# Gate products side by side, the convolutions' end spread over steps, and result rows in 4 KB pieces

## The chip, the cores and the metric

The kernel runs on one core of one Trainium2 chip. The metric is device time in microseconds (us) for one execution, lower is better. The core has five engines with an instruction queue each, and each works through its queue in order: TensorE (PE, matrix products; its weight loads are shown apart as PEld), VectorE (DVE), ScalarE (ACT), GpSimd (POOL) and SyncE (SP, which here only issues transfers). Matrix products land in PSUM, of which this kernel uses eight tiles of 128 x 512 float32 in turn; all other tiles lie in SBUF. The engines wait for one another by semaphores, and 16 DMA engines move data between HBM and SBUF. Everything is float32.

## The reference, cut to what matters

Four images of 256 channels and 32 x 32 places (1024 tokens each) pass through a "metaformer" layer and then through a mixture of eight experts, of which each token uses two.

```python
def _L0_conv_ref(x, ...):
    xn = layernorm(xs, norm_w, norm_b)                     # per token, over 256 channels
    xm = mamba_v(xc, ...) + skip_scale * xc                # 4 groups of 64 channels: a scan over 1024 tokens
    Q = conv1d(conv1d(x_concat, qdw_w, qdw_b, groups=NB, pad=1), qpw_w, qpw_b, groups=1, pad=0)
    g = jax.nn.sigmoid(Q)                                  # 4 gates per token
    xg = (g[...] * xm) ...                                 # each group of 64 channels times its gate
    R = conv1d(conv1d(xgt, rdw_w, rdw_b, groups=Cc, pad=1), rpw_w, rpw_b, ...) + xgt
    cat = concatenate([xs, R])
    xm2 = conv1d(conv1d(cat, fdw_w, fdw_b, groups=2 * Cc, pad=1), fpw_w, fpw_b, ...) + cat[:, :Cc, :]
    x_local = conv1d(xm2, lc_w, lc_b, groups=Cc, pad=1)
    x_global = mha(xm2, ...)                               # 8 heads
    x_out = gelu(layernorm(concatenate([x_local, x_global]) @ fc_w.T + fc_b, lgn_w, lgn_b))
    ...                                                    # depthwise 3x3, norm, projection

x = x + _L0_conv_ref(_ln_c(x), ...)
t = _to_tokens(x)
t = t + _L0_ffn_ref(_ln_t(t), ...)     # top 2 of 8 experts, each gelu(x W1 + b1) W2 + b2
x = _from_tokens(t, x)
```

The first convolution of `Q` takes three neighbouring tokens and the 64 channels of a group to one value per group, so 256 channels to 4; the second takes 4 to 4.

## The kernel before

The program is one interleaving made by hand. Pieces of work are Python generators; `yield n` says "go on n steps later", and `beat()` lets one step pass. A step of the scan is one pair of DVE instructions (`dBu`, then the scan `hs`), a part is 16 steps (one group of one image, one half of its tokens), and an image has eight parts. I write part 1.2 for part 2 of image 1. While image b is scanned in parts b.0 to b.3, `convolutions(b - 1)` runs beside it; after part b.3 the scan pauses for `attention(b - 1)`. The last image's convolutions, attention and norms run after the scan, between tiles of the experts (256 rows each); the remaining tiles follow, and `bring_back` ends the program.

```python
        def step(b, n, h, i):                                   # one step of the scan
            dBu = ps(...)
            nc.vector.tensor_tensor(dBu, dts[g][:, 1, :], bs[q], ALU.mult)
            nc.vector.tensor_tensor_scan(hs, dA[i], dBu, 0.0 if h == 0 else last, ALU.mult, ALU.add)
            ...
            nc.gpsimd.tensor_tensor(hs, hs, cs[q], ALU.mult)
        # dA is made on ACT three steps ahead (LEAD = 3); bs on PE from step g == 1 of the quarter before
        # yp (sums of hs) on PE; up, zp, dtp, cp, op are the projections of the neighbouring parts
...
        def in_turn(items, make, use, lag=2):
            made = []
            for at in range(len(items) + lag):
                if at >= lag:
                    use(items[at - lag], made[at - lag])
                if at < len(items):
                    made.append(make(items[at]))
                yield 1
...
        def normalised(b):
            ...
            for c in range(NC2):
                xl = a4(f"xl_{b}_{c}")
                nc.gpsimd.tensor_tensor(xl, xn[:, c, LEFT:], r1, ALU.mult)
                yield 1
                nc.vector.tensor_tensor(xn[:, c, LEFT:], xn[:, c, LEFT:], r2, ALU.mult)
                ...
        def convolutions(b):
            ...                                                  # d[0]: depthwise of xs, for fp
            qs, qd = [], []
            for h in range(2):
                qd.append(ps(f"qd_{b}_{h}"))
                for i in range(6):
                    c, k = divmod(i, 3)
                    nc.tensor.matmul(
                        qd[h][0:NB], qdwT_s[:, c, k, :], xm[:, c, ds(k + h * HALF, HALF)],
                        start=(i == 0), stop=(i == 5),
                    )
                    if i % 3 == 2:
                        yield 1
            for h in range(2):
                yield 1 - h
                qs.append(a2(f"qs_{b}_{h}", NB))
                nc.scalar.activation(qs[h], qd[h][0:NB], AF.Identity, bias=...)
            yield 1
            # gate(c): gp = qpwT_s x qs, two products of 4 rows; sigmoid(c, gp): g on ACT, with a table
            # load before and after; then xm = g * xm (POOL), depthwise d[1] of xm (ACT, DVE, DVE),
            # rp = rpwT x d[1] (PE) added to xm (DVE), depthwise d4r of xm, and then:
            yield from in_turn(
                CO_H, lambda at: product(f"fp_...", fpwT_s, at[0], [...]), mixed,
            )                                                     # 4 items of 4 products; mixed: DVE
            yield from prepared(b)                                # vp and qkp, for the attention
...
    def bring_back(self, b, m2):
        y = m2.tile([P, NT, C], F32, tag="yy", name=f"yy_{b}", bufs=self.B)
        for h in range(2):
            nc.sync.dma_start(
                y[:, ts(h, NT // 2), :],
                self.Y[ds(b * N + h * HALF, HALF), :].rearrange("(t p) c -> p t c", p=P),
            )
        o = m2.tile([P, NC2, N], F32, tag="o", name=f"o_{b}")    # two buffers
        for h in range(2):
            for c in range(NC2):
                op = self.psum.tile(...)
                for t in range(NT // 2):
                    nc.tensor.transpose(op[:, ts(t, P)], y[:, h * (NT // 2) + t, ts(c, P)], self.ident)
                if c: nc.scalar.copy(o[:, c, ts(h, HALF)], op)
                else: nc.vector.tensor_copy(o[:, c, ts(h, HALF)], op)
            nc.scalar.dma_start(self.out[b]..., o[:, :, ts(h, HALF)])
```

## Time and profile before

| | |
|---|---|
| time | 2474.78 us, median of 3 runs (2465.03 to 2476.65) |
| span of the profiled execution | 2472.8 us |
| scan and what lies beside it | 60.6 to 1657.9 us |
| last image's convolutions to routing, with expert tiles between | 1657.9 to about 2145 us |
| expert tiles alone | about 2145 to 2436 us |
| loading, turning and storing the result | 2436 to 2472.8 us |
| busy over the span | PE 2134.3, DVE 1632.3, ACT 1194.4, POOL 1101.3 us |
| mean granted clock of PE | 0.906 |

A line of the timeline gives start, duration, engine, source line, operation, output and inputs, shapes, and in brackets how long the engine had been idle before and what released it. A line of the windows gives a stretch, its length, the busy time of PE, PEld, DVE, ACT and POOL with the number of instructions, the granted PE clock, the busy share of the DMA engines and what they moved. A float32 product shows as two records, so "x8" is four products. A busy PE is not a PE at its peak, and a wait for several semaphores is put down to the one that the profile shows last.

### The profile page before, as it was taken

The numbers are of one execution on the slowest core, as the hardware profiler recorded it, in microseconds if no ns is written. First come the engines' busy times: TensorE is split into PE (matmuls) and PEld (weight loads), VectorE is DVE, ScalarE is ACT, GpSimd is POOL, SyncE is SP. The second block draws the span as 40 slices with busy tenths as digits, with TensorE's granted clock in tenths as the row PEclk, the third lists the DMA queues.
The fourth block names the chain that finished last, engine by engine and source line by source line (L and its number), as shares of the span: only waits on it lengthen the run. The fifth ranks groups of instructions, "written<-read, shape, count | busy, mean of one in ns | idle before, by whom it ended". The sixth has DMA issues, their size and how long they took to land. (4 is left out here: it accounts for less than half of the span.)

```text
span 2472.8 us, 28317 instructions
## 1 busy us (share of the span) xinstructions
PE 2134.3 (86%) x8810; PEld 947.7 (38%) x8810; DVE 1632.3 (66%) x2255; ACT 1194.4 (48%) x2019; POOL 1101.3 (45%) x1182
## 2 busy tenths in 40 slices
PE   7767768999977799987689999658999889899995
PEld 2111112322211132222123223114752568788885
DVE  3989898875898977789878787985525154211111
ACT  4554445468654548764254786325258533122221
POOL 0777776632676850366776205571130012322221
PEclk7888888899998899988788999768999989899997
DMA  3534433220334230043322202342340155766665
GB/s 90 138 99 111 99 95 78 60 56 27 74 94 108 72 76 26 22 115 91 112 74 57 48 18 59 88 154 88 90 124 1 45 152 162 211 197 193 193 197 157
DMA packets 154980, 244.30 MB, mean 99 GB/s; under 512 B 34184, under 2 KB 103452, under 8 KB 154816
## 3 DMA queue, kind: packets, MB, share of 16 engines
q1 hardware_dynamic: 135640, 217.05, 31.0%
q0 software_dynamic: 13264, 17.85, 3.7%
q10 hardware_dynamic: 5912, 7.45, 0.9%
q8 instruction: 74, 1.21, 0.2%
q14 instruction: 90, 0.74, 0.1%
HBM read 141.16 MB, written 33.98 MB: 71 GB/s over the span
## 5 line engine op out<-in xcount | busy, mean ns | idle before, releaser
L607 POOL TENSOR_TENSOR hs<-hs,cs 128x512 f32<-128x512 f32 x512 | 669.6, 1309 | 213.1 <-DVE hs L602 168.9
L613 PE MATMUL yp<-hs,quads 128*32 128x512 f32 x1024 | 342.3, 702 | 157.6 <-POOL hs L607 113.1
L588 ACT ACTIVATE dA<-dts,A 128x512 f32<-128x512 f32 x512 | 342.1, 713 | 276.3 <-DMA dts<-dt 194.4
L595 DVE TENSOR_TENSOR dBu<-dts,bs 128x512 f32<-128x512 f32 x512 | 347.8, 679 | 64.8 <-ACT u L517 13.3
L1896 POOL DMA_INDIRECT Y<-ys,dest x70 | 112.2, 1602 | 562.0 <-DVE ys L1890 555.5
L602 DVE TENSOR_TENSOR_SCAN hs<-dA,last,dBu 128x512 f32<-128x512 f32 x256 | 327.6, 1280 | 24.9 <-DVE dBu L595 0.5
L602 DVE TENSOR_TENSOR_SCAN hs<-dA,dBu 128x512 f32<-128x512 f32 x256 | 312.4, 1220 | 35.0 <-ACT dA L588 9.4
L928 ACT ACTIVATE e<-st 128x512 f32<-128x512 f32 x512 | 263.0, 606 | 90.0 <-PE st L918 89.1
L1875 ACT ACTIVATE hs<-h,b 128x256 f32<-128x256 f32 x280 | 116.8, 471 | 388.1 <-PE h L1870 233.0
L1880 PE MATMUL y<-w,hs 128*128 128x256 f32 x1120 | 266.1, 390 | 6.9 <-ACT hs L1875 6.9
L1870 PE MATMUL h<-xT,w 128*128 128x256 f32 x1120 | 252.4, 381 | 1.2 <-DVE xT L1848 1.2
L1848 DVE COPY xT<-xp 128x512 f32<-128x512 f32 x35 | 24.2, 691 | 323.5 <-PE xp L1847 308.5
L1880 PEld LDWEIGHTS y<-w,hs 128*128 128x128 f32 x1120 | 217.4, 197 | 46.2 <-issue 9.5
L606 POOL COPY last<-hs 128x1 f32<-128x1 f32 x256 | 66.5, 260 | 372.4 <-DVE hs L602 342.5
L1870 PEld LDWEIGHTS h<-xT,w 128*128 128x128 f32 x1120 | 213.2, 191 | 38.9 <-issue 8.4
L580 PE MATMUL bs<-u,xpwT_s 128*32 128x512 f32 x1024 | 184.9, 692 | 42.9 <-DVE hs L602 23.5
L613 PEld LDWEIGHTS yp<-hs,quads 128*32 128x32 f32 x1024 | 55.8, 120 | 409.5 <-POOL hs L607 271.1
L970 DVE TENSOR_TENSOR e<-e,e 128x512 f32<-128x512 f32 x256 | 171.3, 730 | 54.4 <-ACT e L928 27.6
L918 PE MATMUL st<-qk 32*128 32x512 f32 x1024 | 195.7, 658 | 7.9 <-DVE hs L602 4.5
L496 PE MATMUL up<-xn,inwk 64*128 64x512 f32 x256 | 140.5, 696 | 12.5 <-DVE hs L602 12.4
L960 PE MATMUL av<-e,v 128*32 128x512 f32 x1024 | 142.7, 625 | 0.0
L918 PEld LDWEIGHTS st<-qk 32*128 32x128 f32 x1024 | 68.4, 189 | 135.3 <-issue 89.2
(273 smaller groups left out, 2515.9 us busy)
## 6 DMA issues: line engine op xcount, KB each, us to landing
w<-in_W_dram SPq DMA_DIRECT2D x136, 512.0 KB
dts<-dt SPq DMA_DIRECT2D x512, 128.0 KB
cs<-cd SPq DMA_DIRECT2D x512, 64.0 KB
xs<-XS SPq DMA_DIRECT2D x35, 260.0 KB
b<-in_b_dram SPq DMA_DIRECT2D x35, 128.0 KB
xn<-in_x_dram SPq DMA_DIRECT2D x8, 512.0 KB
XL<-xl SPq DMA_DIRECT2D x8, 512.0 KB
xl<-XL SPq DMA_DIRECT2D x4, 1024.0 KB
```

What stands on the lines that cost most here:

```text
L580: nc.tensor.matmul(bs[r], xpwT_s[:, n, s : s + 1].to_broadcast([P, 32]), T[b, n, "u"][:, half(h)], start=True, stop=True,)
L588: nc.scalar.activation(dA, T[b, n, h, "dts", g][:, 0, :], AF.Exp, scale=A[:, g, n, q : q + 1])
L595: nc.vector.tensor_tensor(dBu, T[b, n, h, "dts", g][:, 1, :], T[b, n, h, "bs", q], ALU.mult)
L602: nc.vector.tensor_tensor_scan(hs, T[b, n, h, "dA", i], dBu, 0.0 if h == 0 else last, ALU.mult, ALU.add)
L607: nc.gpsimd.tensor_tensor(hs, hs, T[b, n, h, "cs", q], ALU.mult)
L613: nc.tensor.matmul(T[b, n, h, "yp"][ts(g, 32)], quads, T[b, n, h, "hs", q * GD + g], start=(q == 0), stop=(q == GS - 1),)
L918: nc.tensor.matmul(sts[i], k[r, ts(kt, P)], q[r, half(h)], start=True, stop=not shifted)
L928: nc.scalar.activation(es[i], sts[i], AF.Exp, scale=1.0 / HD**0.5)
L960: nc.tensor.matmul(accs[0][ts(i, HD)], v8[:, kt, ts(4 * g + i, HD)], es[i], start=(kt == 0), stop=(kt == NK - 1),)
L970: nc.vector.tensor_tensor(first[i], first[i], es[i], ALU.add)
L1870: nc.tensor.matmul(hp[:, i, :], w1(c, k), xT[:, c, :], start=(c == 0), stop=(c == NC2 - 1))
L1880: nc.tensor.matmul(yp[:, ts(t, C)], hs[:, k, ts(t, P)], w2(k), start=(k == 0), stop=(k == NHC - 1))
```

## The change

There are five edits.

1. The gate's first products run in four column strips of the array, 32 wide, one for each half of the tokens and each half of the channels, and accumulate over the three taps in one PSUM tile. One activation takes all 128 rows to SBUF. The second product sums the two channel halves through weights that are laid out four times, 32 rows apart, with zeros between; the two token halves use 64 rows of the array each. Weights and bias are cleared by POOL and loaded first among the later weights. The stage takes four steps where it took six.
2. The convolutions' last products (`fp`) are made every second step for images 0 to 2. The aim is that DVE, which uses them, does not wait for PE.
3. `normalised` leaves one step more between POOL's `xl` and the DVE product that follows it on the same tile.
4. In the norms of the last image both roots stand in one step, after a step's pause.
5. `bring_back` loads rows of the result so that each partition gets one piece of 4 KB (four consecutive rows) and no longer four of 1 KB; the copies out of PSUM put the columns back in order, writing every fourth element. The output tile has four buffers, not two.

```diff
--- before.py
+++ after.py
@@ -178,8 +178,11 @@
         aoutT_s = load(aoutT, "aoutT_s")
         projT_s = load(projT, "projT_s")
         fcT_s = load(fcT, "fcT_s")
-        qdwT_s = load(qdwT, "qdwT_s")
-        qpwT_s = load(qpwT, "qpwT_s")
+
+
+        qdwT_s = wp.tile([P, NC2 * 3 * NB + 32 - NB], F32, name="qdwT_s")
+        qpwT_s = wp.tile([P, C], F32, name="qpwT_s")
+        qdw_b = wp.tile([P, 1], F32, name="qdw_b")
         rpwT_s = load(rpwT, "rpwT_s")
         fpwT_s = load(fpwT, "fpwT_s")
         wvT_s = load(wvT, "wvT_s")
@@ -195,6 +198,19 @@
         def later_weights():
 
             nc.sync.dma_start(vb, vbias.rearrange("a (c p) -> p (a c)", p=P))
+            for t in (qdwT_s, qpwT_s, qdw_b):
+                nc.gpsimd.memset(t, 0.0)
+            yield 1
+            nc.sync.dma_start(
+                qdwT_s[:, 0 : NC2 * 3 * NB], qdwT.rearrange("p c k n -> p (c k n)")
+            )
+            yield 1
+            for i in range(4):
+                nc.sync.dma_start(qpwT_s[32 * i : 32 * i + NB, :], qpwT)
+                if i % 2 == 0:
+                    at = _AT["qdw_b"]
+                    nc.sync.dma_start(qdw_b[32 * i : 32 * i + NB, :], vecs[0:NB, at : at + 1])
+                yield 1
             for t, ap in later:
                 nc.sync.dma_start(t, ap)
                 yield 1
@@ -373,15 +389,15 @@
                 )
             return out
 
-        def in_turn(items, make, use, lag=2):
-
-            made = []
+        def in_turn(items, make, use, lag=2, every=1):
+
+            made, lag = [], lag // every
             for at in range(len(items) + lag):
                 if at >= lag:
                     use(items[at - lag], made[at - lag])
                 if at < len(items):
                     made.append(make(items[at]))
-                yield 1
+                yield every
 
         CO_H = [(co, h) for co in range(NC2) for h in range(2)]
 
@@ -471,7 +487,7 @@
             for c in range(NC2):
                 xl = a4(f"xl_{b}_{c}")
                 nc.gpsimd.tensor_tensor(xl, xn[:, c, LEFT:], r1, ALU.mult)
-                yield 1
+                yield 2
                 nc.vector.tensor_tensor(xn[:, c, LEFT:], xn[:, c, LEFT:], r2, ALU.mult)
                 yield 1
                 nc.sync.dma_start(XL[b][:, c, :], xl)
@@ -750,30 +766,28 @@
                 yield 1
             xm = XM.pop(b)
 
-            qs, qd = [], []
-            for h in range(2):
-                qd.append(ps(f"qd_{b}_{h}"))
-                for i in range(6):
-                    c, k = divmod(i, 3)
+
+
+            qd, qs = ps(f"qd_{b}"), a2(f"qs_{b}")
+            for k in range(3):
+                for i in range(4):
+                    h, c = divmod(i, 2)
                     nc.tensor.matmul(
-                        qd[h][0:NB], qdwT_s[:, c, k, :], xm[:, c, ds(k + h * HALF, HALF)],
-                        start=(i == 0), stop=(i == 5),
+                        qd[ts(i, 32)], qdwT_s[:, ds((3 * c + k) * NB, 32)],
+                        xm[:, c, ds(k + h * HALF, HALF)],
+                        start=(k == 0), stop=(k == 2),
                     )
-                    if i % 3 == 2:
-                        yield 1
-            for h in range(2):
-                yield 1 - h
-                qs.append(a2(f"qs_{b}_{h}", NB))
-                nc.scalar.activation(
-                    qs[h], qd[h][0:NB], AF.Identity, bias=col("qdw_b", 0, slice(0, NB))
-                )
+                yield 1 if k else 0
+            yield 1
+            nc.scalar.activation(qs, qd, AF.Identity, bias=qdw_b)
             yield 1
             def gate(c):
                 gp = []
                 for h in range(2):
                     gp.append(ps(f"gp_{b}_{c}_{h}"))
+                    r = ts(h, 64)
                     nc.tensor.matmul(
-                        gp[h], qpwT_s[:, ts(c, P)], qs[h], start=True, stop=True
+                        gp[h], qpwT_s[r, ts(c, P)], qs[r], start=True, stop=True
                     )
                 return gp
 
@@ -821,7 +835,7 @@
                 CO_H, lambda at: product(
                     f"fp_{b}_{at[0]}_{at[1]}", fpwT_s, at[0],
                     [d[ci // 2][:, ci % 2, half(at[1])] for ci in range(4)],
-                ), mixed,
+                ), mixed, every=1 if b == B - 1 else 2,
             )
             yield from prepared(b)
 
@@ -1013,9 +1027,10 @@
                 for h in range(2):
                     yield 1
                     var.append(column_mean(f"var_{name}_{h}", sq[h]))
+                yield 1
                 for h in range(2):
-                    yield 1
                     root(r[:, half(h)], var[h], eps5)
+                yield 1
             else:
                 for h in range(2):
                     sq = squares(h)
@@ -1909,11 +1924,12 @@
         nc, NT = self.nc, self.NT
         y = m2.tile([P, NT, C], F32, tag="yy", name=f"yy_{b}", bufs=self.B)
         for h in range(2):
+
             nc.sync.dma_start(
                 y[:, ts(h, NT // 2), :],
-                self.Y[ds(b * N + h * HALF, HALF), :].rearrange("(t p) c -> p t c", p=P),
-            )
-        o = m2.tile([P, NC2, N], F32, tag="o", name=f"o_{b}")
+                self.Y[ds(b * N + h * HALF, HALF), :].rearrange("(p t) c -> p t c", p=P),
+            )
+        o = m2.tile([P, NC2, N], F32, tag="o", name=f"o_{b}", bufs=self.B)
         for h in range(2):
             for c in range(NC2):
                 op = self.psum.tile([P, HALF], F32, tag="ps", name=f"op_{b}_{c}_{h}")
@@ -1921,10 +1937,12 @@
                     nc.tensor.transpose(
                         op[:, ts(t, P)], y[:, h * (NT // 2) + t, ts(c, P)], self.ident
                     )
+                to = o[:, c, ts(h, HALF)].rearrange("c (p t) -> c t p", t=NT // 2)
+                op = op.rearrange("c (t p) -> c t p", p=P)
                 if c:
-                    nc.scalar.copy(o[:, c, ts(h, HALF)], op)
+                    nc.scalar.copy(to, op)
                 else:
-                    nc.vector.tensor_copy(o[:, c, ts(h, HALF)], op)
+                    nc.vector.tensor_copy(to, op)
             nc.scalar.dma_start(
                 self.out[b].rearrange("(c p) n -> p c n", p=P)[:, :, ts(h, HALF)],
                 o[:, :, ts(h, HALF)],
```

## The prediction

> **What bounds the kernel now.** I read the page first, then DVE's waits in the timeline, then windows cut at the stages. The page (busy sums, then tenths in 40 slices):
>
> ```profile
> PE 2134.3 (86%) x8810; PEld 947.7 (38%) x8810; DVE 1632.3 (66%) x2255; ACT 1194.4 (48%) x2019; POOL 1101.3 (45%) x1182
> ...
> PE   7767768999977799987689999658999889899995
> PEld 2111112322211132222123223114752568788885
> DVE  3989898875898977789878787985525154211111
> ```
>
> Two engines take turns. Slices 2 to 8 are DVE's: a step of the scan costs 0.68 + 1.25 = 1.93 us there (the page's mean of `dBu` and of the scan), and 16 of them, a part with nothing beside it, 31 us. In the attention (around slice 9), and from slice 28 on, PE has little idle time. So I windowed image 1: parts 1.0, the gap before 1.1, 1.1, the start of 1.2, the rest of 1.2 and 1.3, the attention:
>
> ```profile
> 344.00:383.00 39.00, 30.75 (x83) 7.85 (x84) 36.34 (x38) 20.28 (x29) 30.15 (x37) 0.87 0.40 106
> 383.00:387.50 4.50, 4.50 (x24) 1.10 (x23) 0.73 (x2) 2.08 (x4) 1.38 (x2) 1.00 0.51 144
> 387.50:431.70 44.20, 34.83 (x104) 8.93 (x104) 40.66 (x42) 23.91 (x34) 31.94 (x23) 0.81 0.28 66
> 431.70:443.80 12.10, 6.95 (x27) 1.30 (x27) 11.72 (x13) 9.57 (x15) 9.09 (x11) 0.82 0.10 29
> 443.80:514.40 70.60, 69.19 (x228) 26.43 (x228) 58.82 (x64) 32.13 (x51) 44.21 (x44) 0.93 0.33 80
> 514.40:611.80 97.40, 97.30 (x622) 28.84 (x622) 57.63 (x78) 74.19 (x146) 16.53 (x11) 0.96 0.09 30
> ```
>
> Up to 443.8 DVE sets the pace (PE idles 5 of 12 us just before); from there to the end of the attention PE is busy for 166.5 of 168 us. DVE's waits that the change aims at:
>
> ```profile
> 185.77 2.28 DVE L475 TENSOR_TENSOR xn<-xn,r 128x1024 f32<-128x1024 f32 x1 [3.09 <-POOL xl L473]
> ...
> 386.73 0.70 DVE L595 TENSOR_TENSOR dBu<-dts,bs 128x512 f32<-128x512 f32 x1 [3.87 <-DMA cs<-cd]
> ...
> 390.38 0.70 DVE L595 TENSOR_TENSOR dBu<-dts,bs 128x512 f32<-128x512 f32 x1 [1.63 <-ACT g L785]
> ...
> 467.55 0.75 DVE L818 SCALAR_TENSOR_TENSOR xl<-fp,V,xl 128x512 f32<-128x512 f32 x1 [4.51 <-PE fp L362]
> ...
> 474.81 0.75 DVE L818 SCALAR_TENSOR_TENSOR xl<-fp,V,xl 128x512 f32<-128x512 f32 x1 [4.65 <-PE fp L362]
> ```
>
> The 3.87 us are put down to a transfer, but `dBu` does not read `cs`; it reads `bs`, whose products stand behind the twelve `qd` on PE and end at about 386.6. The end of the kernel:
>
> ```profile
> 1657.90:1693.00 35.10, 27.26 (x70) 10.49 (x70) 29.67 (x35) 14.54 (x20) 4.18 (x6) 0.84 0.59 203
> 1693.00:1720.00 27.00, 24.04 (x69) 14.09 (x70) 7.92 (x15) 13.24 (x17) 7.70 (x5) 0.83 0.12 20
> 1720.00:1960.00 240.00, 238.52 (x1208) 128.34 (x1207) 92.68 (x196) 123.25 (x232) 32.86 (x48) 0.99 0.22 67
> 1960.00:2200.00 240.00, 209.98 (x932) 175.21 (x931) 86.05 (x237) 75.36 (x141) 61.94 (x74) 0.93 0.58 170
> 2200.00:2436.00 236.00, 235.57 (x1125) 207.09 (x1123) 41.09 (x129) 54.47 (x130) 51.53 (x48) 1.00 0.62 178
> 2436.00:2472.80 36.80, 12.08 (x64) 10.71 (x64) 6.17 (x12) 4.68 (x8) 3.22 (x3) 0.64 0.73 239
> ```
>
> DVE leads until 1693 (the 3x3 convolution of image 2), PE from 1720, DMA in the last 26 us.
>
> **What the Trainium skill says.** "TensorE: Matmul & The Clock Gate", Part 3, measured 3.07x for four 32-row tiles and 2.38x for three 32-column tiles. The trace agrees: four `bs` in column strips take 1.07 us, four products in turn (`up`) 3.70. "ScalarE: Activation LUTs", What ACT_TABLE_LOAD costs, gives about 1283 ns for a load; so does the trace (1283 mean over 39), and a sigmoid needs two. "DMA: Bandwidth & Descriptors", Why small descriptors are slow, names a fixed cost per packet; the trace's packet records have medians of 46 ns for 1 KB, 84 for 2 KB and 159 for 4 KB, so 4 KB in one piece cost 159 ns and in four 184. "Perfetto Trace Analysis", Optimization Strategy, advises to find the gaps of the engine that matters, regime by regime; hence the windows.
>
> **The change part by part.**
>
> *Gate products.* `qd`: 12 products an image at 0.94 us (page: 45.2 us busy for 48) become 3 rounds of four at about 1.07: 11.3 to 3.2 us. `gp`: 4 at 1.08 to about 2.0. PE saves 10.4 us an image. In the quarter where `qd` stands, PE had 17 us of work against 7.7 of DVE; now about 9. Lead absorbs that, so the 3.9 us gap goes, and likely the 1.6 (`dBu` needs a PSUM tile that `gp` holds) and 0.5 us waiting for `yp`: 6.0 an image.
>
> But two steps less make ACT the next limit. In the changed program's order on ACT stand, after the silu block, `dA` `qs` `dA` `dA` `dA`, then load-`g`-`g`-load, `dA`, load-`g`-`g`-load, `dA`, four for `dt`, two `dA`, and the first `d` of `rdw`. From the trace (back to back: `dA`, `qs` 0.65, `g` 0.63, load 1.28, the four 2.45, `d` 1.24): starting at 380.9 as before, five at 0.65 end at 384.1, load-`g`-`g`-load (3.8) at 388.0, `dA` and the second block at 392.4, `dA` of step 4 of part 1.1 at 393.1, the four and two `dA` at 396.8, `d` at 398.1. DVE, no longer held, comes from 381.65 by four and a half steps at 1.93 and `y` (0.75) to that `dA` at 392.2, and after the scan to `d` at 394.3, so it waits 0.9 + 3.8 = 4.7 us, an estimate. Before, two steps more and the gap itself hid this. The start is 0.6 us earlier, as `up` stands behind eight packed `qd` (2.2 us) and no longer three (2.8).
>
> *Spread of `fp`.* From 443.8 on PE is saturated whatever DVE does: 443.8 is where `yp` of step 1.2/3 is let go, and after it come in either order the same `fp` (15 us), `up` (7.4), `vp`, `qkp` and attention. DVE's 9.2 us of waiting are its slack there, not the kernel's time. Spreading moves the wait and brings nothing, except that PE's 1.3 us of waiting for DVE at the attention's start (0.45 + 0.87) may vanish. As the convolutions run two steps ahead until `fp`, one more `d4r` (1.4 us) lies before 443.8.
>
> Each of images 0 to 2: -6.0 + 4.7 - 0.6 + 1.4 - 1.3 = -1.8 us. Three: **-5**.
>
> *`normalised`.* Only image 1's runs where DVE leads. One step (1.9 us) more for POOL cuts 3.1 to about 1.2, and the 1.3 us wait before it: **-3**. The others run in the attention or in parts without such waits.
>
> *Last image.* 10.4 us of PE work go, but before 1693 DVE is the limit, so most of it becomes idle time. After 1693 PE has `gp` of one half less and the other packed (about 2.8 us), and of its 3 us of idle time until 1720 perhaps a third goes, as the gates come some 8 us earlier: **-4**. The convolutions end before expert tile 4 and not in its middle, so one tile moves from before the attention to the end; PE leads in both places, 14.3 us each: 0. The two roots: 0.
>
> *Results.* 4 MB read and written: 4096 packets of 1 KB took 12.7 us per DMA engine. As 1024 of 4 KB, 12.7 x 159/184 = 11.0: -1.7. Four output buffers take away the wait at 2460.7 (6 us on the timeline, DMA share down to 0.86 and 0.59, so about 1.1 us of transfers lost): together **-3**. The strided copies have as many elements.
>
> *Weights.* Eight short loads more and three clears, one per step: 0.
>
> Sum: -5 - 3 - 4 - 3 = -15, so 2474.8 - 15 = 2460. The reading of ACT is my least certain step and errs towards too little gain, so I take 2457.
>
> **Rivals.**
> 1. *ACT does not become the limit.* If `g` is ready early enough, the three images give 6.5 us each and the sum is about -30: 2445. For it: ACT is busy 46 to 54% of the windows from 344 to 431.7. Against: 17 us of extra ACT work stand in some eight steps.
> 2. *DVE's waits on `fp` count in full.* Then 9 us for each of three images come on top: 2460 - 27 = 2433. For it: the waits are plain. Against: PE's 1.4 us of idle time in 70.6.
> 3. *The shift costs.* The moved tile puts the first tile of a new series, which now waits 6 to 7 us for its rows at 2001 and 2159, in a worse place, or the transposed stage finds DVE slower: 0 to +5 us, 2475 to 2480.
> 4. *PE gets more clock.* Granted clock is 0.81 to 1.00 in these windows and its rule is not visible; a few us either way.
>
> **Range and chances.** Rivals 1 and 2 set the low end, 3 the high end, and the three runs before spread by 0.5%: 2436 to 2472. Over 2% faster means under 2425.3, which needs rivals 1 and 2 together: 0.05. Slower by 2% has no source: 0.02. Within 2%: 0.93.
>
> **What would show it.** In the changed profile: `qd` busy about 13 us and not 45; no gap before parts 1.1, 2.1 and 3.1; instead DVE waiting some 4 us for ACT (`d`) in 1.1; waits for `fp` still there, and 443.8's counterpart to the attention's end within 2 us of 168; image 1's 3.1 us wait down to about 1; the last stage 3 us shorter. I am wrong if the stretch from part 1.2's fourth step to the attention's end shrinks by over 3 us, if no ACT wait appears, or if the time from the scan's end to the first load of results does not fall, or falls by over 9 us.

## The result, and the profile after

The changed kernel needs 2446.97 us (median of 4 runs, 2441.18 to 2449.26), the kernel before 2471.09 us (4 runs, 2465.03 to 2476.65). The ratio is 0.9899, with a 95% interval of 0.9866 to 0.9932. That is 24 us less, inside the predicted range of 2436 to 2472 and 10 us under the predicted 2457. The sum was nearly right. Three of its terms were not, as the experiments show.

The page of the changed kernel, busy sums and tenths in 40 slices, as shown of before:

```profile
PE 2073.0 (85%) x8810; PEld 929.7 (38%) x8810; DVE 1634.0 (67%) x2255; ACT 1192.6 (49%) x2013; POOL 1098.3 (45%) x1185
...
PE   7767767999976799987769999667999989899995
PEld 2211111332211132222113323114733667788884
DVE  3989998876899988789988877985443343211111
```

PE is busy 61 us less. The gate products took away 41 of these: `qd` went from 45.2 to 12.6 us of busy time, `gp` from 17.3 to 9.2. The other 20 us are products that were there before and took less time, which the sums do not explain. The windows over image 1 begin to, cut where the prediction cut them (part 1.0, part 1.1, the start of 1.2, the rest of 1.2 and 1.3, the attention; the gap before 1.1 is gone). Columns: stretch, length, then busy us of PE, PEld, DVE, ACT, POOL, the granted PE clock, DMA share and GB/s.

```profile
341.00:379.80 38.80, 29.07 (x112) 8.13 (x112) 37.00 (x39) 21.08 (x30) 30.73 (x38) 0.87 0.41 109
379.80:425.80 46.00, 31.23 (x99) 6.68 (x96) 40.27 (x43) 26.17 (x36) 32.02 (x24) 0.82 0.30 76
425.80:438.45 12.65, 7.22 (x27) 1.23 (x27) 12.35 (x13) 7.93 (x13) 10.63 (x11) 0.86 0.06 22
438.45:504.90 66.45, 65.95 (x228) 25.97 (x228) 57.18 (x63) 31.31 (x48) 43.30 (x44) 0.97 0.35 85
504.90:599.10 94.20, 94.20 (x623) 28.12 (x622) 56.16 (x77) 75.06 (x149) 14.04 (x11) 1.00 0.09 31
```

Part 1.0 and the gap: 43.5 to 38.8 us. Part 1.1: 44.2 to 46.0. The last two lines are the stretch that the prediction held to be fixed PE work: 168.0 us before, 160.65 now. PE has hardly any idle time in either and the same instructions in both, give or take one record. What differs is the clock column: 0.93 and 0.96 before, 0.97 and 1.00 now. DVE's waits in image 1, from the timeline (in brackets: idle time before, and the releaser):

```profile
382.64 0.70 DVE L611 TENSOR_TENSOR dBu<-dts,bs 128x512 f32<-128x512 f32 x1 [1.56 <-ACT g L799]
394.06 2.27 DVE L411 SCALAR_TENSOR_TENSOR d<-xm,V,d 128x1024 f32<-128x1024 f32 x1 [2.74 <-ACT d L406]
...
459.66 0.75 DVE L832 SCALAR_TENSOR_TENSOR xl<-fp,V,xl 128x512 f32<-128x512 f32 x1 [3.84 <-PE fp L378]
466.92 0.75 DVE L832 SCALAR_TENSOR_TENSOR xl<-fp,V,xl 128x512 f32<-128x512 f32 x1 [2.74 <-PE fp L378]
```

Of the two waits for ACT in part 1.1 the second, for `d`, is a new one and was predicted. The first stands before the second `dBu` of the part and ends with `g`, as the 1.63 us of before did, which the prediction had expected to go. The waits for `fp` are 6.58 us together, where they were 9.16 (and 6.55 in the kernel before run once more, below). The end of the kernel, from the first copy of a result tile to the last instruction, first before and then after:

```profile
2449.60:2472.80 23.20, 10.84 (x60) 9.43 (x58) 5.34 (x8) 4.68 (x8) 0.00 (x0) 0.65 0.86 303
```

```profile
2412.00:2439.40 27.40, 10.44 (x60) 9.18 (x58) 8.14 (x8) 8.16 (x8) 0.00 (x0) 0.69 0.70 259
```

This end became 4.2 us longer, and it moves 259 GB/s in place of 303. The copies' busy time rose from 5.34 and 4.68 us to 8.14 and 8.16.

### The profile page after: what moved, and what is told of

Read it like the earlier page. It is cut to its first block, busy times and chain, and to the rows that moved or that the text cites. A ratio compares the mean times of both kernels' runs of the same rounds, so it can differ in the third digit from the quotient of the medians.

```text
span 2439.4 us, 28277 instructions
## 1 busy us (share of the span) xinstructions
PE 2073.0 (85%) x8810; PEld 929.7 (38%) x8810; DVE 1634.0 (67%) x2255; ACT 1192.6 (49%) x2013; POOL 1098.3 (45%) x1185
## 5 line engine op out<-in xcount | busy, mean ns | idle before, releaser
L932 PE MATMUL st<-qk 32*128 32x512 f32 x1024 | 189.0, 649 | 4.6 <-ACT e L942 4.4
L512 PE MATMUL up<-xn,inwk 64*128 64x512 f32 x256 | 135.5, 674 | 10.8 <-DVE hs L618 10.7
```

The costliest lines, as they stand in the source:

```text
L932: nc.tensor.matmul(sts[i], k[r, ts(kt, P)], q[r, half(h)], start=True, stop=not shifted)
```

## The experiments

The theories: **A**, the schedule and the PE work decide, and the clock varies on top of them; **B**, DVE's waits for `fp` count in full; **C**, short pauses of PE cost through the clock that is granted after them. Every run below was timed beside the kernel before on the same chip. Ratios are to that kernel, with 95% intervals; one thousandth is 2.5 us.

### The kernel before, once more (e1_same)

No edit.

> The kernel before, unchanged, to see how its granted clock and its time go together. Both profiles so far differ in clock (0.906 before, 0.918 after), and in the changed kernel's four runs the time falls from 2449.3 us at 0.910 to 2441.2 at 0.918, about 1 us for each 0.001. Theory A (the work decides, and the clock differs from run to run on top): ratio 0.998 to 1.002, the runs spread over some 8 to 12 us and lie on a line of about -1 us per 0.001 of clock, and at 0.912 the old kernel would need about 2468. Theory C (the change itself raises the clock): the old kernel's runs all stay at 0.904 to 0.908, below every run of the changed one (0.910 to 0.918).

Measured: 1.0000 (0.9988 to 1.0011), 14 runs of 2466.5 to 2478.7 us. Their clocks run from 0.904 to 0.912, and the time falls by 0.9 us for each 0.001 of clock. So A is right that the clock varies from run to run of one kernel, and that the time goes with it: 0.008 of clock is some 7 of the 12 us between the fastest and the slowest run. In its profile part 0.6 took 32.0 us with 10 us at half clock. In the profile of before it was 36.0 with 24, and in that of the changed kernel 32.0. So these 4 us are not a gain of the change.

### The packed gate products alone (e2_gates)

Edit: the first point of the change alone, with its weight loads.

```diff
-            qs, qd = [], []
-            for h in range(2): ...        # 12 products of 4 columns, six steps
+            qd, qs = ps(f"qd_{b}"), a2(f"qs_{b}")
+            for k in range(3): ...        # 3 rounds of four 32-column strips, four steps
```

> The kernel before with the packed gate products alone (and the weight loads that they need). Theory A: the gaps before parts 1.1, 2.1 and 3.1 go (4.6 us each), the new waits for ACT in parts 1.1, 2.1, 3.1 take 2 to 3 us of each back, and parts 0.0 and 0.1 get some 4 us longer because the folding of the weights comes later beside the scan; the end of the last image's convolutions gains 1 us at most: together -2 to -7 us, 2464 to 2469, ratio 0.997 to 0.999. The two waits of DVE for fp in part 1.2 stay at about 4.5 us each. Theory C (fewer narrow gate products keep PE's clock up): the stretch from part 1.2's yp to the end of the attention falls from 172.5 to about 166 us with less than 10 us of it at half clock, and the whole is 2450 to 2458.

Measured: 0.9985 (0.9973 to 0.9997), about -4 us. Against the profile of before, parts 1.0, 2.0 and 3.0 (with the gap behind them) are 4.5, 4.5 and 6.3 us shorter; 1.1, 2.1 and 3.1 are 1.8, 3.7 and 1.6 longer; 1.2, 2.2, 3.2 are 3.9, 2.7 and 2.5 shorter; and from part x.3 to the attention's end all three are longer, by 3.2, 3.6 and 3.3 us. That last loss fits a saturated PE: DVE reaches part x.3 earlier, and the attention ends no earlier for it. To the attention's end the three images gain 3.4, -0.1 and 3.9 us. The last image gains more than I expected: from the scan's end to the first copy of the results 782.4 us in place of 791.4 in the run before. And the weights lose: from part 0.0 to 0.2 it takes 73.9 us in place of 67.2. (Together the profiles give some 9.5 us and the runs 4: the profiled execution of before was 2.2 us slower than the median of its runs, that of this run 3.4 us faster.) In part 0.1 stands a new wait (same view as above):

```profile
102.13 0.70 DVE L611 TENSOR_TENSOR dBu<-dts,bs 128x512 f32<-128x512 f32 x1 [4.54 <-DMA qk_b<-in_vecs_dram]
```

`dBu` does not read `qk_b`. The products that fold the weights stand ahead of `bs` on PE, and they wait for loads that are now issued some steps later. The stretch from part 1.2's `y` to the attention's end stayed at 171.4 us, so the gate products are not what raised the clock there. One thing theory A had not expected: DVE's waits for `fp` in part 1.2 did not stay at about 4.5 us each. They shrank to 2.30 us together, as the `fp` products now stand closer together on PE. DVE idles elsewhere instead (11.7 us in all from `y` to its last scan before the attention, 11.9 in the profile of before), and PE's three pauses at the attention's start, the last three lines, are the ones that it has without the edit:

```profile
460.06 0.75 DVE L832 SCALAR_TENSOR_TENSOR xl<-fp,V,xl 128x512 f32<-128x512 f32 x1 [0.78 <-PE fp L378]
463.49 0.75 DVE L832 SCALAR_TENSOR_TENSOR xl<-fp,V,xl 128x512 f32<-128x512 f32 x1 [0.76 <-PE fp L378]
466.92 0.75 DVE L832 SCALAR_TENSOR_TENSOR xl<-fp,V,xl 128x512 f32<-128x512 f32 x1 [0.76 <-PE fp L378]
...
513.40 1.12 PE L932 MATMUL st<-qk 32*128 32x512 f32 x2 [0.42 <-DVE hs L618]
515.36 1.77 PE L932 MATMUL st<-qk 32*128 32x512 f32 x4 [0.84 <-DVE hs L618]
517.36 1.99 PE L932 MATMUL st<-qk 32*128 32x512 f32 x4 [0.23 <-DVE hs L618]
```

The next run shows what these pauses mean.

### The spread alone (e3_spread)

```diff
-                    [...],
-                ), mixed,
+                    [...],
+                ), mixed, every=1 if b == B - 1 else 2,
```

> The kernel before with fp spread over twice as many steps, alone. Theory A: the saturated stretch (from the yp of part 1.2's third step to the end of the attention, 172.5 us of which 20.5 at half clock in the kernel before, that is 162.3 at full clock) keeps 161 to 163 us at full clock, the waits on fp shrink to 2.5 to 4 us each without the end moving, and the time is 2466 to 2474, ratio 0.998 to 1.001. Theory B (DVE's waits on fp count): 5 to 7 us for each of three images, 2450 to 2456, ratio 0.991 to 0.994, with the stretch shorter at full clock too. Theory C (the spread raises the clock, because full-size products then stand nearer to the point at which PE has no more idle time): the same 2450 to 2458, but with the stretch unchanged at full clock and its time at half clock down from 20 to 6 to 12 us.

Measured: 0.9916 (0.9900 to 0.9932), -20.8 us. This is most of the whole change, and A's "same" is refuted. The same stretch (from part 1.2's `y` to the attention's end) in the kernel before once more, and then with the spread:

```profile
436.60:606.50 169.90, 165.53 (x852) 54.44 (x852) 120.89 (x144) 108.35 (x200) 64.73 (x59) 0.96 0.19 51
```

```profile
438.80:602.30 163.50, 161.10 (x854) 53.58 (x852) 120.47 (x146) 108.87 (x200) 64.67 (x59) 0.97 0.20 53
```

6.4 us here, and 7.5 and 6.1 in images 2 and 3, worked out in the same way: 20 in all. PE's idle time fell from 4.4 to 2.4 us and its busy time from 165.5 to 161.1, for the same products. DVE's waits for `fp` are 3.15 us, where they were 9.16 in the first profile of before and 6.55 in the one shown here. B would explain the gain with them, but the changed kernel has 6.58 us of such waits and a stretch of 165.4 us, 4.5 less than here with as many. With the spread:

```profile
468.37 0.75 DVE L818 SCALAR_TENSOR_TENSOR xl<-fp,V,xl 128x512 f32<-128x512 f32 x1 [2.29 <-PE fp L362]
473.85 0.75 DVE L818 SCALAR_TENSOR_TENSOR xl<-fp,V,xl 128x512 f32<-128x512 f32 x1 [0.86 <-PE fp L362]
```

Where the two kinds of time meet is the start of the attention. PE's timeline there, the kernel before once more:

```profile
503.82 1.13 PE L918 MATMUL st<-qk 32*128 32x512 f32 x6
505.39 1.09 PE L918 MATMUL st<-qk 32*128 32x512 f32 x2 [0.44 <-DVE hs L602]
507.35 1.72 PE L918 MATMUL st<-qk 32*128 32x512 f32 x6 [0.87 <-DVE hs L602]
509.26 2.02 PE L918 MATMUL st<-qk 32*128 32x512 f32 x2 [0.19 <-DVE hs L602]
511.22 1.93 PE L960 MATMUL av<-e,v 128*32 128x512 f32 x8
```

and with the spread:

```profile
505.77 3.01 PE L918 MATMUL st<-qk 32*128 32x512 f32 x16
508.71 1.45 PE L960 MATMUL av<-e,v 128*32 128x512 f32 x8
```

Each `st` needs a PSUM tile, and the tiles come free when DVE's last scans (`hs`) have read their `dBu`. DVE is late with them, so PE, which had made it wait, now waits for it. The same eight products take 7.4 us in place of 2.9. How late DVE is does not follow from the length of its waits for `fp`: its last scan before the attention ends 5.4 to 5.5 us after PE's first `st` in all seven profiles without the spread, be the waits 2.3 us (e2) or 9.2, and 1.8 or 2.7 us after it with the spread, be they 3.2 or 6.6. It fits the order of the work. From DVE's last wait for `fp` on DVE has 39.6 us to its last scan, and PE 34.3 us to its first `st` (first profile of before, from 474.8). With the spread that `fp` comes later among DVE's steps: 33.7 and 31.9 us (from 473.9).

Then the clock falls. The windows of the first profile of before are cut here at the moments at which the clock record may change (steps of 3.41 us); the last column but two is the clock:

```profile
511.10:514.51 3.41, 2.35 (x9) 0.63 (x7) 3.15 (x3) 2.00 (x5) 2.06 (x2) 1.00 0.68 176
514.51:521.34 6.83, 6.83 (x26) 1.61 (x26) 1.05 (x2) 1.53 (x3) 1.49 (x2) 0.50 0.54 183
521.34:524.75 3.41, 3.41 (x31) 1.05 (x31) 3.19 (x4) 2.86 (x6) 1.48 (x2) 1.00 0.00 0
```

An interval with PE busy for 2.35 of 3.41 us is followed by two at half clock with PE busy throughout, 26 records of `st`, `av` and `yp` in 6.83 us where the next interval has 31 in 3.41. In seven profiles without the spread (this kernel twice and five of its variants) all 21 attentions of images 0 to 2 begin with 3.4 to 10.2 us at half clock. In the six with the spread none does.

### Adding work to fill the pauses (f1_fill)

The decisive test of C: nothing is taken from the kernel before, and products without a use are added. (Four throwaway products are written into the first `st` tile and overwritten.)

```diff
                 sts = [ps(f"st_{b}_{g}_{h}_{kt}_{i}") for i in range(4)]
+                if b < B - 1 and (g, h, kt) == steps[0]:
+                    for _ in range(4):
+                        nc.tensor.matmul(
+                            sts[0], wqkT_s[:, 0, 0, :], q[:, half(h)], start=True, stop=True
+                        )
```

> The kernel before, with work added and nothing removed: at the start of the attention of images 0, 1 and 2 (beside the scan of the next image) four throwaway products of 128 by 128 by 512 (0.47 us each, 1.9 us together, written into the first st tile and overwritten by it). They fill the three short pauses (0.45, 0.87 and 0.20 us in the profile of before) after which the clock fell to a half for 6.8 us in every profile without the spread. Theory C (the pauses cost through the clock): no half-clock stretch at the attention's start, so +1.9 - 1.5 - 3.4 = -3.0 us for each of three images, about -9 us, 2461 to 2467, ratio 0.995 to 0.998: more work, less time. Theory A (only work and waits count): +0.4 us each, +1 us in all, up to +6 if the pauses stay, ratio 1.000 to 1.0025.

Measured: 0.9963 (0.9950 to 0.9975), -9 us. I had reckoned 1.9 us for the four products, which is one record for each; each is two, they took 3.70 us, and the kernel is still faster. PE's timeline, and a window over it:

```profile
503.76 3.70 PE L918 MATMUL st<-qk,wqkT_s 128*128 128x512 f32 x8
507.39 2.99 PE L923 MATMUL st<-qk 32*128 32x512 f32 x16
510.31 1.46 PE L965 MATMUL av<-e,v 128*32 128x512 f32 x8
```

```profile
505.00:516.00 11.00, 11.00 (x66) 3.41 (x68) 7.26 (x9) 6.25 (x13) 5.51 (x5) 1.00 0.60 181
```

The first `av` starts at 510.31, earlier than the 511.22 of the run without added work, whose first `st` began at the same time. No half clock follows here, nor in the other two attentions. DVE's waits for `fp` stay at 6.5 us an image, as in e1. A's +1 us is refuted. The pauses do cost through the clock. (The added products use all 128 rows and `st` uses 32, so the run does not tell whether the length of the pauses counts or the work done in the interval.)

### The last stage: pieces, buffers, both (e4_results, r1_pieces, r2_buffers)

The edit of `bring_back`, whole, then the 4 KB pieces with two buffers, then four buffers with the 1 KB pieces:

```diff
-                ....rearrange("(t p) c -> p t c", p=P),          # e4, r1
+                ....rearrange("(p t) c -> p t c", p=P),
-                nc.scalar.copy(o[:, c, ts(h, HALF)], op)
+                nc.scalar.copy(to, op)                           # to: every fourth element
-        o = m2.tile([P, NC2, N], F32, tag="o", name=f"o_{b}")    # e4, r2
+        o = m2.tile([P, NC2, N], F32, tag="o", name=f"o_{b}", bufs=self.B)
```

> The kernel before with the last stage's 4 KB pieces and four result buffers alone. Theory A: the last stage falls from 36.8 to about 32.4 us as in the changed kernel and nothing else moves: -3 to -5 us, 2466 to 2468, ratio 0.998 to 0.999. Rival D (the stage is held by the bytes moved, and what was gained there in the changed kernel came from the rows ending at another moment): under 1.5 us.

> The kernel before with the results loaded in 4 KB pieces and written transposed with a stride, but with the old number of result buffers. In the run with the whole edit the strided copies took 1.08 us on VectorE and 1.09 on ScalarE in place of 0.69 and 0.58, and the loads 11.7 us of each DMA engine in place of 12.6. Theory E (the strided copies cost more than the pieces save): +1 to +3 us, ratio 1.0004 to 1.0012. Theory F (the loss is in the buffers alone): -1 to -2 us, ratio 0.999.

> The kernel before with four result buffers, but with the old 1 KB pieces. In the run with the whole edit ScalarE stood 6.1 us in the issue of two stores, where before it waited for a buffer. Theory E: the stores were limited by the transfers anyway, so four buffers change the end by -1 to +0.5 us, ratio 0.9995 to 1.0002. Theory F (issuing early fills the queue, ScalarE stands in the issue and cannot copy): +2 to +4 us, ratio 1.001 to 1.0015. The prediction had -1.1.

Measured: both 1.0015 (1.0006 to 1.0025), +4 us; the pieces alone 1.0025 (1.0015 to 1.0034), +6 us; the buffers alone 1.0001 (0.9991 to 1.0012). So this edit costs time, and it is the pieces with their strided copies that cost. The copies' groups, before and then with the whole edit (busy, mean ns of one, idle time before and what ended it):

```profile
L1927 DVE COPY o<-op 128x512 f32<-128x512 f32 x8 | 5.3, 689 | 23.5 <-PE op L1921 15.1 <-DMA out_dram<-o 6.0 <-SPq L68 2.4
L1925 ACT COPY o<-op 128x512 f32<-128x512 f32 x8 | 4.7, 585 | 32.1 <-DMA yy<-Y 21.0 <-DMA out_dram<-o 5.3 <-PE op L1921 2.0
```

```profile
L1928 ACT COPY o<-op 128x512 f32<-128x512 f32 x8 | 8.2, 1100 | 28.8 <-PE op L1922 22.1 <-DMA out_dram<-o 6.2 <-ACT o L1928 0.5
L1930 DVE COPY o<-op 128x512 f32<-128x512 f32 x8 | 8.1, 1077 | 25.9 <-PE op L1922 15.1 <-DMA out_dram<-o 5.4 <-SPq L68 5.4
```

A copy that writes every fourth element takes 1100 ns on ACT and 1077 on DVE, not 585 and 689. The loads did get cheaper, 11.7 us of each DMA engine in place of 12.6 (packet records of both profiles), but DMA then has gaps. ACT, which issues the stores, stands in the issue of two of them. With the pieces alone:

```profile
2457.67 6.51 ACTq L1931 DMA_DIRECT2D out_dram<-o  x2
```

Before, two issues took 1.1 us, and a later copy waited 5.3 us for a buffer:

```profile
2453.67 1.11 ACTq L1928 DMA_DIRECT2D out_dram<-o  x2
...
2460.68 0.58 ACT L1925 COPY o<-op 128x512 f32<-128x512 f32 x1 [5.27 <-DMA out_dram<-o]
```

Four buffers alone brought nothing. How much of the loss is the copies' and how much the issue's was not separated.

### The changed kernel without that edit (g1_noresults)

> The changed kernel without its edit of the last stage. If the parts add up (packed gates -4, spread -20, last stage +4, the rest small), this is 2472.6 - 24 - 4 = 2443 to 2447, ratio 0.988 to 0.990, some 3 us faster than the changed kernel, and the stage after the first result load is as short as before (23 us from the first copy to the end, and not 27). If the edit of the last stage pays beside the packed gates, this is slower than the changed kernel: 2449 to 2452.

Measured: 0.9883 (0.9864 to 0.9901), 2445.19 us. This is as expected if the parts add up, but its interval overlaps that of the changed kernel, and the 2 to 4 us between them are not shown by these two runs alone.

### One step more in the normalisation (e5_norm)

```diff
                 nc.gpsimd.tensor_tensor(xl, xn[:, c, LEFT:], r1, ALU.mult)
-                yield 1
+                yield 2
```

> The kernel before with one step more between POOL's xl and VectorE's xn in the normalisation, alone. The prediction: VectorE's waits in part 0.3 (1.33 and 3.09 us) fall to 0 and 1.2, -3 us, ratio 0.9985 to 0.9990. In the changed kernel the second was 2.51 and the part 3.1 us shorter. Rival (image 0's length is set by its clock and the shift only moves the wait): within 1 us, ratio 0.9996 to 1.0004.

Measured: 0.9990 (0.9980 to 1.0000), about -2.5 us. Part 0.3 fell from 42.2 to 39.1 us. The first wait is gone, and the second went from 3.09 only to 2.50. In the same profile part 0.4 took 36.0 us in place of 32.2, with 24 us at half clock, as part 0.6 did in the profile of before. So the gain rests on the runs, and their interval reaches to zero:

```profile
186.18 2.27 DVE L475 TENSOR_TENSOR xn<-xn,r 128x1024 f32<-128x1024 f32 x1 [2.50 <-POOL xl L473]
```

### Three versions further (b1_late, b2_steps, b3_fill2)

All stand on the changed kernel without its edit of the last stage. b1 moves the packed weights' loads behind the folding; b2 also gives the gates two steps back; b3 is b1 with throwaway products in part x.2.

```diff
             nc.sync.dma_start(vb, ...)
-            for t in (qdwT_s, qpwT_s, qdw_b): ...               # b1, b2, b3: this block goes
-            ...                                                  # to the generator's end
-                yield 1 if k else 0                              # b2
+                yield 1
-            yield 1                                              # b2, after qs
+            yield 2
             bs = T[b, n, h, "bs", q] = ps(...)
+            if b > 0 and (n, h) == (1, 0) and q in (1, 2):       # b3
+                for _ in range(4):
+                    nc.tensor.matmul(bs, wqkT_s[:, 0, 0, :], u..., start=True, stop=True)
```

> The changed kernel without its edit of the last stage, and with the eight loads and three clears for the packed gate weights put behind the folding of the other weights, where nothing waits for them. In the run with the packed gates alone part 1.0 began 6 us later than before. Theory A (the six steps of loads push the folding on VectorE into part 0.1, where it costs about 4 us): image 0 is 4 to 6 us shorter, the rest as in the run without the last stage's edit (0.9883): 2438 to 2442, ratio 0.986 to 0.987. Rival (the folding costs the same wherever it stands, and the 6 us were the granted clock): within 1.5 us of 0.9883.

> As the run with the late weights, with two steps more in the gates (one between the rounds of products, one after the copy to qs), as many as the kernel before had. Theory A (the loss in parts 1.1, 2.1, 3.1 comes from the gates' work on ScalarE standing too close together): the waits for d and dBu there fall from 4.3 to under 1.5 us an image and the time by 2 to 3 us for each of three, 2431 to 2436, ratio 0.983 to 0.985. Rival (PE's work from part x.2 on ends the image, so what VectorE gains in x.1 comes back in the attention, as in the run with the packed gates alone, where 3.9 us gained in x.2 came back as 3.2): within 2 us of the run with the late weights.

> As the run with the late weights, with twice four throwaway products (1.9 us at full clock each time) into the bs tiles of the second and third quarter of parts 1.2, 2.2, 3.2, where PE pauses for hs and the clock falls before fp. Theory C (pauses cost through the clock): the half-clock time between the start of these parts and their first 20 us falls from 7 to 13 us to under 4, worth 1 to 3 us an image after the added work: ratio 0.984 to 0.986 and under the run with the late weights by 2 to 6 us. Rival (the pauses here lie where VectorE leads, and the added products hold up yp and with it VectorE): 1 to 6 us slower than the run with the late weights.

Measured: b1 0.9860 (0.9839 to 0.9881), 2434.1 us; b2 0.9852 (0.9825 to 0.9878), 2430.8 us; b3 0.9842 (0.9823 to 0.9860), 2429.4 us.

b1: part 0.1 is back at 35.6 us, from 42.9 in e2, and parts 0.0 and 0.1 take 70.2 us together in place of 73.9. The order of the loads mattered, by about 4 us in this view, and its ratio lies 2.3 thousandths under g1's, with overlapping intervals.

b2: the steps given back do not take ACT's delay away. In part 1.1 the wait moved from `d` to `dBu` and stayed as long:

```profile
396.55 0.70 DVE L613 TENSOR_TENSOR dBu<-dts,bs 128x512 f32<-128x512 f32 x1 [4.58 <-ACT g L801]
```

In 2.1 and 3.1 it was 3.79 and 2.05 us, where A expected under 1.5. So A's remedy failed. What gain there is against b1 is within the intervals.

b3: its products add 26 us of busy time to PE (1.9 us each time, so 11, were reckoned), and the time does not rise, as the rival expected. The half-clock time in the first 20 us of parts 1.2, 2.2 and 3.2 fell from 10.2, 7.1 and 13.6 us in b1 to 6.8, 0 and 6.4. C expected a fall, but to under 4 us. Whether it is faster than b1 is not decided, as the runs of both overlap. It is the one version whose whole interval lies under that of the changed kernel.

## Why the prediction was right, and where it was wrong

The total was right, but partly because errors offset one another. Each part's run gives its term (the ratio times 2472 us; 2469 for the normalisation):

| part | predicted | measured alone |
|---|---|---|
| packed gates, with last image and weights | -5.5 | -4 (-7 to -1) |
| spread of `fp` (the 1.3 us at each attention) | -4 | -21 (-25 to -17) |
| normalisation | -3 | -2.5 (-5 to 0) |
| last stage | -3 | +4 (+1.5 to +6) |
| sum | -15.5 | -23.5 |

The four terms measured alone add up to about the -24 to -25 us of the whole change. Their intervals leave some 6 us either way, so nothing shows that the parts act on one another, and nothing excludes it. The fourth edit, the roots, was not run alone.

*Gate products, right in the main.* `qd` to 12.6 us of busy time (about 13 predicted); no gap before parts 1.1, 2.1, 3.1, worth 4.5 to 6.3 us each (6.0 predicted); and ACT becomes the next limit: DVE waits 2.74 us for `d` (3.8 predicted). The predicted 0.9 us for `dA` did not appear. In their place stand 1.56 us for `g`, a wait that was there before with 1.63 and was to go. So the waits for ACT in part 1.1 add up to 4.3 us, near the predicted 4.7, by luck. (The prediction's own terms for the 0.9, from 381.65 four and a half steps and `y`, also give 391.1 and not 392.2, so they should have given 2.0.) Rival 1 fell with the wait for `d`. Two terms of this part were mis-sized and offset one another. The last image gained 9.0 us and not 4, for PE's busy time there fell by 14 us (736.0 to 721.8 over the windows from the scan's end to the first copy) and not only in the places that I had counted. And "Weights: 0" was wrong: 6.7 us, as the folding products stood behind the new loads and held up `bs`.

*Spread, wrong.* The step that failed is "DVE's 9.2 us of waiting are its slack there, not the kernel's time. Spreading moves the wait and brings nothing", except 1.3 us. The observation under it stands: PE's products are the same, and PE is busy nearly all the time. That DVE's waits for `fp` are not the kernel's time stands too, as the changed kernel has as many of them as e1 in a shorter stretch. But the conclusion took PE's busy time for work at one speed, and PE's own 1.3 us of waiting at their face value. DVE hands back the PSUM tiles that the attention begins with. Without the spread its last scan ends 5.4 us after PE's first `st`, PE pauses, and 3.4 to 10.2 us at half clock follow; with the spread it ends 1.8 or 2.7 us after it, and there is no pause. The three stretches gained 20 us, 6.7 each, where the prediction had 1.3.

Split by the clock record over the three images' stretches, the 20 us between e1 and e3 are 6.1 us less idle time of PE, 9.6 us less lost to half clock (49 us of busy time at half clock became 30, at half the price) and 4.4 us of shorter records, mostly of `st`, whose ends are modelled; the eight products that filled 7.4 us suggest that waiting hides in these. f1 shows that filling the pauses pays; that the whole of the 20 us came through them is worked out and not shown. Rival 2 had the size, 27 us, from the wrong cause: what counted was not DVE's wait but PE's, and what followed it.

The prediction had put the clock aside as rival 4, "a few us either way, and its rule is not visible". The records that it had already used contained the rule in part. In the profile of before, worked out from the clock record and PE's records, all 62 returns to full clock came after an interval of 3.41 us with PE busy for 82% of it or more, and half of the 63 falls came after intervals with PE busy for 37% or less. But the busy share is not the whole rule. Of the intervals at full clock all 35 with PE busy for less than 40% were followed by a fall, none of 21 with 50 to 60%, and 10 of 55 with 60 to 80%. Six falls came after intervals that PE was busy throughout. Three of these were filled mostly by the `gp` products of four rows, three by the products of the experts' gate, which are 8 columns wide. In the six profiles with packed gate products no interval at full clock with a `gp` product is followed by a fall. So a record's length does not say how much its product counts for the clock.

"TensorE: Matmul & The Clock Gate", Part 1, The HAM clock gate, describes two states, half and full clock, decided in windows of about 3.4 us that run freely whatever the program does. The trace agrees in the two values and in the 3.41 us. It differs on the cause: the page's table of the two states asks for an idle window, and here one with PE busy for 69% was enough.

*Normalisation, right in sum.* The first of the two waits did go, the second fell to 2.5 and not to 1.2. Part 0.3 is 3.1 us shorter, and the runs, with -2.5 us and an interval that reaches to zero, agree with the predicted 3 without proving it.

*Last stage, wrong in sign.* The step that failed is "The strided copies have as many elements". They have, and take 1.6 to 1.9 times as long. That the loads would gain was right (0.9 us for each engine, 1.7 predicted), but the loads alone do not set the stage's length, and the buffers' 1.1 us did not appear.

*What would show it.* The stretch held to 168 us shrank by 7.4, beyond the 3 us named. That condition was the right one to set, and it pointed at the wrong step. The time from the scan's end to the first load of results fell by 8.4 us, inside its limits.

## What to carry to other kernels

A saturated engine's busy time is not yet fixed work: look at its granted clock beside its busy share, find the short pauses and the narrow products just before the clock falls, and price a pause with what follows it. When one engine waits for a second, ask what the first will owe the second a little later, above all PSUM tiles, and compare the work that each has left until then; the length of the wait does not tell. Before trading a transfer's shape for a strided copy, measure the copy; and when small new loads are put in front of old ones, look at who waits for the old ones.

## What the runs showed of the hardware

- Three pauses of PE, 1.5 us by the records, preceded 6.8 us at half clock. Added products of 3.70 us in their place made each of the three stretches shorter (by 2.6, 3.9 and 3.4 us), and the kernel 9 us faster.
- PE can be busy throughout an interval of 3.41 us by its records and be given half clock in the next: six times in the profile of before, after products of four rows or of 8 columns.
- The clock differs from run to run of one program: e1's 14 runs lie between 0.904 and 0.912, and their time is 0.9 us shorter for each 0.001 more. In three of the later profiles (g1, b2, b3) part 0.2 ran 33 us at half clock and took 47.6 us, in all others but one 39 to 40 (43.7 with 20 us at half clock in e3's). Such an event is larger than most terms of the prediction, so parts of two profiles are compared only with their clock beside them.
- A copy from PSUM of 128 x 512 with every fourth element written took 1100 ns on ACT and 1077 on DVE, against 585 and 689 with the elements in order.
